# One planned order or the order of writing: the attention of a two-block kernel behind its scans

## The chip, the cores and the metric

The kernel runs on one core of a Trainium2 chip. The metric is the device time of one execution in microseconds (us); the figure given for a kernel is the median of its runs. A core has five engines with an instruction queue each: PE (TensorE, matrix products), DVE (VectorE), ACT (ScalarE), POOL (GpSimd) and SP (SyncE), which here issues nearly all DMA transfers. Engines meet through semaphores: an instruction can wait for another engine's or a DMA's.

## The reference

The input `x` is `[4, 96, 128, 128]` in float32. Two blocks follow each other, each on a group-normalised input and each added to its input.

Block 0 is a selective scan: a 1x1 product to 192 channels, a depthwise 3x3 convolution, SiLU, four scans over the image's pixels (rows, columns, and both backwards) with input-dependent decay, a layer norm over the channels and a product back to 96 channels.

Block 1, the one that the change concerns, in the reference's words:

```python
def _attn_conv(x1, x2, aw1, aw2, aw3):
    key = _unfold_nonoverlap(_conv2d(x1, aw1, pad), K).reshape(B, C, kk, -1)
    qry = _unfold_nonoverlap(_conv2d(x2, aw2, pad), K).reshape(B, C, kk, -1)
    attn = jnp.einsum('bckl,bqkl->bqck', key, qry)
    attn = jax.nn.softmax(attn.reshape(B, C, C * kk) / sqrt(C * kk), axis=2)
    value = _conv2d(x1, aw3, pad)
    return jax.vmap(lambda v, w: _conv2d(v[None], w, pad)[0])(value, w_attn)
...
xr, x1, x2 = _relu_split_norm(x, sc1, sc2, res_coef, nc1, nc2)
y1 = _layer_norm(_attn_conv(x1, x2, aw1, aw2, aw3))
y2 = _layer_norm(_conv2d(x2, w_conv2, K // 2)) * x1
return xr + _conv2d(jnp.concatenate([y1, y2], axis=1), w_full, 0) + b_full[None, :, None, None]
```

`_relu_split_norm` splits the normalised input into its positive part `x1` and negative part `x2`, each normalised with statistics over the whole image.

## The kernel before

**Stages.** The program first runs block 0: projections of the four images, and the scans (`ssm_scan`) over pairs of images. Beside the last scans it computes, for images 0 and 1, the scan output (`ssm_output`) and the norm (`split_norm`). Then block 1 follows image by image, `attention(img)`. While image b is in `attention`, a second generator runs beside it: the output of image b-1 (`attn_output`, by `close`), and, for b = 1 and 2, `ssm_output` and `split_norm` of image b+1. The output of image 3 runs alone at the end.

**How two stages are put side by side.** Each stage is a Python generator that emits instructions and yields a cost. `co_run(left, right, pace)` (line 275) takes a step of `left`, and then steps of `right` until these have cost `pace` times as much. In the attention the pace is 0.6 (line 1706). The order in which the Python code creates instructions is the order of emission.

**Attention.** An image has 11 strips of 12 rows. In a strip, two maps are convolved: `x1` (weights of key and value together) and `x2` (weights of query and `w_conv2` together), each in two chunks of 6 rows (q = 0, 1). The convolution uses four products for each pair of columns. For a chunk:
- `load_rows` (L1184 to L1195) loads rows in six DMAs, into one of two buffers;
- `columns`, a *turn* (L1201): sums and differences of neighbouring columns, on DVE (L1212 to L1214, L1219, L1221) and on POOL (L1212 to L1214), into one of three buffers;
- `products` (L1227): four PSUM banks, two large matmuls each (L1236), and then four small ones (L1247);
- `outputs` (L1262), a *combination*: ACT copies a bank (L1285), DVE forms two columns from four banks (L1277 to L1280), followed by statistics (L1377, L1508) and stores (L1392, L1412, L1509).

After the chunks q = 0 and 1, a third one (q = 2) does the remaining 64 output channels of both. Channels of key and query go into rings in SBUF. Whenever 9 rows are whole, *side pieces* follow the next chunks: transposes of the rings (`turned`, L1337, L1342) and the product of key and query (`multiplied`, L1352, added up by L1362). After 11 strips come softmax and the attention's weights, and then 22 chunks of the value convolution, whose order is the same (`wa` in place of `wd`).

The emission of a chunk is pipelined by hand. The turn of the next chunk comes first; then two matmuls for each bank, and between the banks `later.tick()` emits the copy, the combination, and the load and store that belong to earlier chunks. The banks come from a pool of six, `psa`; the work beside them has two others.

**What sets the order.** The program is written with a framework that tracks the dependences, and plans: it orders each engine's instructions by the emission and by what its own model of the durations holds ready, so an instruction that was emitted later may stand ahead of one emitted earlier. `in_order` (line 312) takes that freedom away for a part of the program: it makes every instruction depend on the one that was emitted before it on its engine. The dependence needs no semaphore, since an engine's own queue keeps its order.

```python
for i in traced()[first:]:
    if i.engine in before:
        tc.add_manual_dep(i, before[i.engine].name, ...)
    before[i.engine] = i
```

`first` is set at line 1670, after the projection of image 0. In the kernel before, `in_order(first)` is called at line 1691, so it covers the projections of images 1 to 3, the scans and what runs beside them. The attention, lines 1692 to 1709, is ordered by the planner.

**Output.** `attn_output` (L1515) begins with statistics (L180 to L190, L1536 to L1563: some 25 small operations, DVE, PE and ACT in turns), and goes on with 16 steps: three loads (L1569), ACT (L1578, L1582, L1588), DVE (L1583, L1584, L1589, L1590), and twice two matmuls (L1594, L1595) with a DVE addition (L1596), then a store (L1598).

Of the kernel before, what the change touches and what calls it, by code (L numbers as in the profile page):

```python
# [60 lines left out]
def kernel(  # L61
# [247 lines left out]
    def traced():  # L309
        return nc.cur_bb.bb.instructions  # L310

    def in_order(first):


        before = {}
        for i in traced()[first:]:
            if i.engine in before:
                tc.add_manual_dep(
                    i,
                    before[i.engine].name,  # L320
                    mybir.DependencyInfo(
                        mybir.DependencyClass.NoSync, mybir.DependencyReason.DATA
                    ),
                    reason="order of emission",
                )
            before[i.engine] = i
# [5 lines left out]
    def drain(gen):  # L332
        for _ in gen:
            pass
# [1328 lines left out]
    with tc.tile_pool(name="wp", bufs=1, side="left") as wp:  # L1663
# [6 lines left out]
        first = len(traced())  # L1670
# [17 lines left out]
    co_run(left, last, 1.6)  # L1688
    drain(left)
    drain(last)  # L1690
    in_order(first)
    early.close()
    psl = ctx.enter_context(tc.tile_pool(name="psa", bufs=6, space=PSUM, side="left"))
    psr = ctx.enter_context(tc.tile_pool(name="psr", bufs=2, space=PSUM, side="right"))
# [2 lines left out]
    for b in range(NB):  # L1697
# [9 lines left out]
        drain(left)  # L1707
        drain(light)
    drain(imgs[NB - 1].close(psr, "right"))


# [73 lines left out]
```

## Time and profile before

| what | value |
|---|---|
| median of 3 runs | 7653.22 us (7650.29 to 7659.47) |
| the profiled execution | 7650.29 us, span 7648.4 us |
| busy: PE, DVE, ACT, POOL | 5837.3 us, 5475.6 us, 3049.4 us, 3141.6 us |
| mean granted PE clock | 0.839 |

The stages behind the scans, in us from the span's start:

| stage | from | to |
|---|---|---|
| last scan instruction | | 3777 |
| image 0: keys and queries, softmax, values | 3788 | 4567 |
| image 1 (beside it the output of 0, scan output and norm of 2) | 4567 | 5636 |
| image 2 (beside it the output of 1, scan output and norm of 3) | 5636 | 6678 |
| image 3 (beside its first strips the output of 2) | 6678 | 7524 |
| output of image 3 | 7524 | 7648 |

A row of the view of busy time by stretch gives, for a window, how long each engine was executing. A row of the timeline gives start, duration, engine, line, operation, output and inputs; in brackets stands how long the engine had been idle before it, and the engine and instruction, or the DMA, that ended the idle time. A matmul in float32 shows as two records.

### The profile page before, as it was taken

To read this page: it belongs to the slowest core of one execution; us is meant where nothing else is said; L and a number is where in the kernel's file an instruction comes from. 1 tells how busy PE (TensorE), PEld (TensorE's weight loads), DVE (VectorE), ACT (ScalarE), POOL (GpSimd) and SP (SyncE) were. 2 spreads that over 40 slices of the span, in tenths; PEclk is the share of its full clock that TensorE was granted. 3 is DMA by queue.
4 is the path that set the end of the run, shared out by engine and by line. 5 is a ranking of instruction groups with operands and counts; after the bars stand their busy time and mean duration, and the time that the engine had idled before them with its cause. 6 is when DMAs were issued, how large, how long until landed. Compare 5 with 4: busy or idle time off the path is not lost. (4 is left out here: it accounts for less than half of the span.)

```text
span 7648.4 us, 72313 instructions
## 1 busy us (share of the span) xinstructions
PE 5837.3 (76%) x21940; PEld 2294.8 (30%) x21940; DVE 5475.6 (72%) x7531; ACT 3049.4 (40%) x3645; POOL 3141.6 (41%) x1826
## 2 busy tenths in 40 slices
PE   4989978789977535553588789987679886798877
PEld 1322322223211101110144433334334343344432
DVE  2248568788867795789866687457877567887678
ACT  1257566677854575376411102304213124121112
POOL 2038457668665465456722242112331112422231
PEclk9999989989965556655599899998899987899998
DMA  4566666766756655855544456586666776665445
GB/s 115 127 155 183 176 184 179 208 169 185 202 155 188 193 166 160 230 154 160 158 129 109 108 157 177 150 213 172 188 171 181 184 194 192 174 180 144 108 139 170
DMA packets 744604, 1279.07 MB, mean 167 GB/s; under 512 B 191654, under 2 KB 465730, under 8 KB 731736
## 3 DMA queue, kind: packets, MB, share of 16 engines
q1 hardware_dynamic: 742024, 1274.18, 60.5%
q8 instruction: 175, 2.87, 0.2%
q14 instruction: 213, 1.74, 0.1%
q0 software_dynamic: 2192, 0.27, 0.0%
HBM read 911.28 MB, written 295.13 MB: 158 GB/s over the span
## 5 line engine op out<-in xcount | busy, mean ns | idle before, releaser
L1236 PE MATMUL bank<-t,wd 128*128 128x384 f32 (+3 forms) x5632 | 1581.1, 512 | 289.8 <-DVE s L1278 118.4
L596 PE MATMUL bank<-y,wp 128*128 128x512 f32 (+3 forms) x3584 | 1323.5, 624 | 71.6 <-DMA y<-y 27.6
L1212 POOL TENSOR_TENSOR t<-y 128x768 f32<-128x768 f32 (+1 forms) x264 | 427.3, 1619 | 2285.8 <-PE bank L1236 1096.7
L826 POOL TENSOR_TENSOR y<-y,dl 128x1024 f32<-128x1024 f32 x384 | 1057.5, 2754 | 657.3 <-DVE dl L818 603.8
L770 PE MATMUL pBC<-xr,wbc 60*128 60x512 bf16 (+1 forms) x1536 | 651.0, 470 | 751.7 <-DVE dA L814 665.7
L793 POOL TENSOR_TENSOR dl<-dl,u 128x1024 f32<-128x1024 f32 x384 | 1034.0, 2693 | 463.1 <-ACT dA L761 293.9
L1285 ACT COPY s<-bank 128x384 f32<-128x384 f32 (+2 forms) x360 | 167.4, 465 | 2436.8 <-PE bank L1247 2318.8
L1236 PEld LDWEIGHTS bank<-t,wd 128*128 128x128 f32 (+1 forms) x5632 | 765.9, 176 | 1033.7 <-issue 610.9
L814 DVE TENSOR_TENSOR_SCAN dA<-dA,pBC 128x512 f32<-128x512 f32 x768 | 981.5, 1278 | 33.7
L818 DVE TENSOR_TENSOR dl<-dA,pBC 128x512 f32<-128x512 f32 x768 | 528.5, 688 | 298.1 <-PE pBC L770 225.6
L596 PEld LDWEIGHTS bank<-y,wp 128*128 128x128 f32 (+3 forms) x3584 | 460.8, 169 | 757.9 <-issue 646.3
L637 ACT ACTIVATE dl<-pd,dtb 128x512 f32<-128x512 f32 x768 | 485.6, 683 | 385.9 <-PE pd L744 382.7
L1236 PE MATMUL bank<-t,wa 128*96 128x384 f32 (+1 forms) x1408 | 494.3, 497 | 182.0 <-DVE s L1278 104.7
L797 DVE TENSOR_TENSOR pBC<-dl,pBC 128x512 f32<-128x512 f32 x768 | 526.6, 686 | 36.6 <-PE pBC L770 36.6
L1277 DVE TENSOR_TENSOR d<-s,bank 128x384 f32<-128x384 f32 (+2 forms) x360 | 191.9, 533 | 496.1 <-ACT s L1285 336.6
L770 PEld LDWEIGHTS <-wbc 60*128 60x128 bf16 (+1 forms) x1536 | 130.0, 103 | 1338.0 <-issue 1334.6
L1212 DVE TENSOR_TENSOR t<-y 128x768 f32<-128x768 f32 (+1 forms) x264 | 302.7, 1146 | 202.3 <-PE bank L1236 175.2
L761 ACT ACTIVATE dA<-dl,negA 128x1024 f32<-128x1024 f32 x384 | 420.2, 1141 | 2.3
L637 ACT ACT_TABLE_LOAD x239 | 306.6, 1283 | 264.8 <-PE pd L744 262.1
L1236 PEld LDWEIGHTS bank<-t,wa 128*96 128x96 f32 x1408 | 219.9, 168 | 451.1 <-issue 433.3
L744 PE MATMUL pd<-xr,wdt 60*128 60x512 bf16 (+1 forms) x768 | 308.8, 485 | 53.6 <-ACT dl L637 40.2
L969 PE MATMUL bank<-y,outws 96*96 96x512 f32 x512 | 340.3, 812 | 11.5 <-DMA y<-yms 11.4
(240 smaller groups left out, 7964.0 us busy)
## 6 DMA issues: line engine op xcount, KB each, us to landing
u<-zb SPq DMA_DIRECT2D x192, 1024.0 KB
y<-yms SPq DMA_DIRECT2D x128, 768.0 KB
xr<-xdt SPq DMA_DIRECT2D x768, 72.0 KB
yms<-y SPq DMA_DIRECT2D x96, 512.0 KB
xn<-xnew SPq DMA_DIRECT2D x128, 384.0 KB
y<-y SPq DMA_DIRECT2D x128, 258.2 KB
zb<-z SPq DMA_DIRECT2D x64, 512.0 KB
y<-x1d SPq DMA_DIRECT2D x168, 193.8 KB
```

What stands on the lines that cost most here:

```text
L596: nc.tensor.matmul(blocks(pz[p:e]), lhsT=ws[k][:, d, c : c + e - p], rhs=window(ys[k], at, d, n), start=(i == 0), stop=(i == len(terms) - 1),)
L637: nc.scalar.activation(dst, src, AF.Softplus, bias=bias)
L761: nc.scalar.activation(live[m]["dA"], live[m]["dl"], AF.Exp, scale=negA[:, g % 3, k : k + 1])
L770: nc.tensor.matmul(p, lhsT=wbc[0 : xr.shape[0], steps[n][0] % 3, q], rhs=xr[:, at : at + CH], start=True, stop=True,)
L793: nc.gpsimd.tensor_mul(t, t, u_view(n))
L797: nc.vector.tensor_mul(p, live[n]["dl"][:, bass.ts(half, CH)], p)
L814: nc.vector.tensor_tensor_scan(h, h, p, init, ALU.mult, ALU.add)
L818: nc.vector.tensor_mul(live[n]["dl"][:, sl], live[n]["dA"][:, sl], live[n]["C", half])
L826: nc.gpsimd.tensor_add(v, v, t.rearrange("p (a b) -> p a b", b=W))
L969: nc.tensor.matmul(po, lhsT=outws[:, j], rhs=y[:, j, sl], start=(j == 0), stop=(j == 1))
L1212: eng.tensor_sub(v[:, 0:2], of(y, 0), of(y, 2))
L1236: nc.tensor.matmul(pc[p:e, :n], lhsT=w[:, i, c : c + e - p], rhs=t[k][:, i, :n], start=(k == 0), stop=False,)
```

## The change

The call of `in_order(first)` moves from the end of the scans to the end of the program. The dependences along each engine now cover the attention, the work beside it and the last output too: each engine executes all that follows line 1670 in the order in which the Python code emits it. The same instructions are emitted, with the same pools, loads and sizes.

```diff
     co_run(left, last, 1.6)
     drain(left)
     drain(last)
-    in_order(first)
     early.close()
     psl = ctx.enter_context(tc.tile_pool(name="psa", bufs=6, space=PSUM, side="left"))
     psr = ctx.enter_context(tc.tile_pool(name="psr", bufs=2, space=PSUM, side="right"))
...
         drain(left)
         drain(light)
     drain(imgs[NB - 1].close(psr, "right"))
+    in_order(first)
```

## The prediction

> **What bounds the kernel now.** I read the busy time by stretch first. The change acts only behind the scans (last scan at 3777 us), and the stages there have different limits. Columns: window, length, then busy us (instructions) of PE, PE weight loads, DVE, ACT, POOL, then PE clock, DMA share, GB/s.
>
> ```profile
> 3788.00:4380.00 592.00, 495.54 (x2616) 261.10 (x2616) 385.13 (x605) 72.71 (x132) 172.16 (x151) 0.93 0.45 118
> 4380.00:4567.00 187.00, 141.74 (x537) 61.83 (x537) 160.57 (x250) 12.63 (x25) 75.30 (x59) 0.93 0.53 153
> 4575.00:4822.00 247.00, 222.43 (x813) 94.39 (x814) 194.28 (x258) 59.48 (x69) 60.68 (x48) 0.90 0.62 169
> 4840.00:5174.00 334.00, 299.16 (x1262) 124.42 (x1264) 163.75 (x281) 60.29 (x74) 42.80 (x43) 0.93 0.73 188
> 5201.00:5425.00 224.00, 166.90 (x852) 91.20 (x850) 167.27 (x281) 126.86 (x169) 55.70 (x73) 0.87 0.67 190
> 6920.00:7329.00 409.00, 355.42 (x1915) 190.40 (x1914) 269.68 (x425) 57.72 (x103) 114.49 (x100) 0.93 0.45 119
> ```
>
> Row 1 is the key and query convolutions of image 0, with no other work beside them; row 6 the same for image 3 once the output of image 2 is done. PE is 84 and 87% busy, so PE plus a stall. Row 2 is the value convolution (DVE 86% over the stretch, and almost gapless within it). Rows 3 to 5 are image 1 with, beside it, the output of image 0, the scan output of image 2 and the norm of image 2. Row 4 is PE work (90%).
>
> The timeline of a strip of image 3 shows the stall of rows 1 and 6. PE:
>
> ```profile
> 7125.08 1.48 PE L1236 MATMUL bank<-t,wd 128*128 128x384 f32 x4
> 7129.76 5.80 PE L1236 MATMUL bank<-t,wd 128*128 128x384 f32 x12 [3.20 <-DVE s L1278]
> ```
>
> and what DVE did meanwhile:
>
> ```profile
> 7122.10 0.96 DVE L1212 TENSOR_TENSOR t<-y 128x768 f32<-128x768 f32 x1 [2.05 <-PE bank L1236]
> 7122.98 1.83 DVE L1213 TENSOR_TENSOR t<-y 128x384 f32<-128x384 f32 x1
> 7124.73 1.18 DVE L1214 TENSOR_TENSOR t<-y 128x384 f32<-128x384 f32 x1
> 7125.83 1.58 DVE L1212 TENSOR_TENSOR t<-y 128x768 f32<-128x768 f32 x1
> 7127.33 0.54 DVE L1277 TENSOR_TENSOR d<-s,bank 128x384 f32<-128x384 f32 x1
> 7127.79 1.36 DVE L1213 TENSOR_TENSOR t<-y 128x384 f32<-128x384 f32 x1
> 7129.08 0.54 DVE L1278 TENSOR_TENSOR s<-s,bank 128x384 f32<-128x384 f32 x1
> ```
>
> The planner has put two column turns (L1212 to L1221) together, and L1278, which frees a PSUM bank, among them. PE stands 3.20 us in each 27.4 us half strip.
>
> One more wait counts, in the timeline at 7012 us: the write into the ring waits for the landing of the store of the chunk before, about 7 us after its issue.
>
> ```profile
> 7011.98 0.56 DVE L1279 TENSOR_TENSOR ring<-s,bank 128x384 f32<-128x384 f32 x1 [5.21 <-DMA c2d<-ring]
> ```
>
> **The Trainium skill.** "PSUM — Partial Sum Buffer", Engine vs sequencer instructions: the queues of ScalarE, VectorE and GpSimd are strictly first in, first out, and matmuls start in program order. So whatever stands ahead of a late instruction in the order costs it the wait; the last row above is an example, 5.21 us in which DVE did nothing else. "SBUF — State Buffer", SBUF: two separate sides: DVE operations with two SBUF inputs and GpSimd operations exclude each other on a shared port pair. The trace agrees: L1213 takes 1.83 us while POOL turns, 0.55 alone. "TensorE: Matmul & The Clock Gate", What's actually happening: after an idle window of some 3.4 us PE runs at half clock. The trace agrees in kind: pairs of L1594 records take 1.02 us in a dense stretch and 2.02 behind a wait at 4609 us.
>
> **The change part by part.** No instruction is added or removed. In the built programs the orders agree up to the attention; behind it, 4971 of DVE's 7469 instructions stand elsewhere, by 13 places on average, PE's and SP's less, POOL's hardly.
>
> *Strips with nothing beside them.* I laid out one strip (two maps, 6 chunks) in the new order with the durations of the rows: 8 matmuls of a chunk 5.35 us, the small ones 0.9, transposes 1.2, the product 1.7, a turn 4.56 (1.24+1.33+0.83+0.54+0.62, means of row 1's stretch), a combination 2.2 (four of 0.55), statistics 1.1, ACT copy 0.5. Where a side piece follows the third chunk, its combination now comes before the next turn: L1278 ends 3.6 us after the third chunk's last large matmul instead of 7. The second turn moves one chunk later. What is late next: in a half strip without side pieces the second turn stands before the first chunk's combination, so PE waits 4 us for that L1278; SP issues six loads (3.3 us) before the ring's store, which lands about 25 us into the half strip, and DVE stands 6 us at L1279. The two halves give 22.7+25.6 = 48.3 us; with about 0.1 us for a dozen handovers, 49.5. Before: 592/11 = 53.8 in image 0 and 409/7.8 = 52.3 in image 3. Gain: 11x4.3 = 47 and 7.8x2.8 = 22. Bounds: PE's own work (495/11 = 45 us a strip) gives 11x8.8+7.8x7.3 = 154; no gain gives 0.
>
> *Start of the first image.* Weights and maps are now issued after the last store of the scans; before, part of the weights went ahead. Some 8 issues at 0.4 to 0.8 us and a longer queue: +10 (0 to 20).
>
> *Image boundaries (three).* Before, the statistics chain of the output (bn_aggr to L1563, 4566 to 4581 us) ran while the new image's rows were loading, and PE's first convolution came at 4580. Now the first turn, which waits for the load to land (4578), stands ahead of that chain on DVE; the chain takes 10 us without what is mixed into it; and the output's own loads stand on SP behind a third row load that waits for that turn. All of PE's convolution is queued behind the first output matmul. +17 each, 51. Bounds: 0 and 30.
>
> *Output beside a convolution (three stages of 247 us).* DVE 194, PE 222. The first output matmul of each of 16 steps (L1595) now waits in place for DVE's L1584, 5 us of ACT and DVE work emitted just before it. In the old order PE could be given convolution meanwhile, and still lost 15 us there. +10 each, 30. Bounds: -10, and 3 us a step, 48.
>
> *Scan output and norm (images 1 and 2).* The scan output's statistics wait for a DMA (about 7 us) at the head of DVE: +8. The norm has two chains of some 20 to 40 small operations (5174 to 5201, 5290 to 5308), now unmixed: +10; but its strips gain as above, -15. The rest, in step with DMA at a share of 0.73: +5. Together +8 each, 16. Bounds: -20 and +40 each.
>
> *Value convolution (four times 187 us).* DVE is full in either order: 0 (-10 to +10 each).
>
> *Last output.* 16 steps, 124 us, DVE 94. SP now issues the next loads behind the store of the finished step, which waits for the last DVE operation: +8 (0 to 25).
>
> Sum: -47 -22 +10 +51 +30 +16 +8 = +46. Own time 7650.29 (span 7648.4): 7696. The median, 7653.22, lies 3 above it.
>
> **Rivals.** *The free strips win* (other side). If the ring's store lands in time and turns are shorter because they no longer collide with POOL, strips run at PE's 45.5 us: -91-53 instead of -69, total 7650+115-144 = 7621. It decides below 47.1 us a strip, where 11x(53.8-p)+7.8x(52.3-p) equals the 115 of losses. For it: row 1's PE idle is 96 us, nearly all behind L1278. Against it: the 5.21 us at L1279.
>
> *The mixed stages lose more.* If each of the 48 output steps costs PE 3 us (+144 instead of 30), and ACT's loads of the norm hold up its copies (64 x 0.5 us = 32): 7696+146 = 7842. For it: rows 3 to 5 have PE and DVE both near full, so strict order couples them. Against it: the planner's progress there (3.1 strips in row 3) is that of the emission order already (3.09 by its pace: 16 steps of 5.2 units over 0.6, at 45 units a strip), so little was rearranged.
>
> *No difference*: gains and losses cancel, 7650.
>
> **How the numbers follow.** A measurement here can tell about 0.2% (15 us). Moderate loss 0.44, strips win 0.24, large loss 0.20, no difference 0.12. Faster 0.24, same 0.12, slower 0.64. Range 7590 to 7810: it takes in the strips' case and most of the large loss. The likeliest case alone: 7666 to 7740.
>
> **What would show it.** Strips of image 0 at 47 to 51 us (key and query convolutions 520 to 560 instead of 592), with L1279 waiting for the ring's DMA more than 24 us in image 0; PE's wait for L1278 down. A boundary from the last value matmul to the first convolution of over 30 us instead of 16. More PE wait at L1595 for L1584 than 63 us. Wrong if free strips come to 46 us or if the mixed stages grow by over 40 us each.

## The result and the profile after

The kernel after takes 7851.08 us (median of four runs, 7843.54 to 7852.16), beside 7656.35 for the kernel before on the same chip: a ratio of 1.0251, interval 1.0233 to 1.0269. The span of its profiled execution is 7849.5 us, and the mean granted PE clock 0.824 instead of 0.839. The forecast was 7696 with a range up to 7810. The sign was as predicted, and so was the split into stages that gain and stages that lose. The size was not: the losses were some three times as large, in part through waits that the prediction did not price, and the time lies outside the range.

Beside the experiments below, the kernel before came to 7651 to 7666 us; a difference of under 15 us between two kernels is not read as one.

Busy time by stretch of the kernel after, with the stages of the rows shown of before, and in the last row the output of image 3 alone (columns as there):

```profile
3787.00:4328.00 541.00, 476.71 (x2580) 249.07 (x2580) 326.68 (x575) 60.41 (x118) 145.27 (x147) 0.95 0.45 121
4348.00:4518.00 170.00, 145.10 (x528) 62.18 (x528) 122.59 (x221) 10.08 (x22) 88.52 (x57) 0.94 0.60 165
4562.00:4814.00 252.00, 201.31 (x773) 88.19 (x772) 188.94 (x241) 62.68 (x68) 45.15 (x35) 0.88 0.58 159
4814.00:5194.00 380.00, 297.91 (x1298) 125.07 (x1297) 180.69 (x302) 62.45 (x79) 49.74 (x50) 0.85 0.68 177
5194.00:5474.00 280.00, 204.02 (x1011) 105.33 (x1010) 189.94 (x336) 135.78 (x178) 59.47 (x84) 0.85 0.61 171
7108.00:7484.00 376.00, 342.48 (x1935) 183.66 (x1919) 235.68 (x426) 47.74 (x93) 100.70 (x103) 0.98 0.46 122
7690.00:7849.50 159.50, 99.41 (x128) 30.51 (x126) 102.03 (x96) 56.43 (x47) 0.00 (x0) 0.67 0.52 143
```

Rows 1 and 6 are shorter, and PE's share rose to 88 and 91%. In rows 3 to 5 it fell to 80, 78 and 73%, where it had been 90, 90 and 75%. So the change does both things, each in its own stages. In the free strips (those with nothing beside them) PE's wait for L1278 fell, and DVE's wait for the ring's store grew. In the view of waits (us in total, times, longest us), image 0 in the kernel before:

```profile
PE bank L1236 <- DVE s L1278: 64.9, 19, 5.7
DVE ring L1279 <- DMA c2d<-ring: 24.3, 4, 7.4
```

and in the kernel after:

```profile
PE bank L1236 <- DVE s L1278: 35.4, 17, 9.5
DVE ring L1279 <- DMA c2d<-ring: 64.2, 9, 9.6
```

In image 3's free strips PE's wait for L1278 fell from 44.5 to 11.7 us; the ring's store is now the longer wait (a strip of image 3, DVE and PE):

```profile
7294.71 0.55 DVE L1278 TENSOR_TENSOR s<-s,bank 128x384 f32<-128x384 f32 x1
7298.63 0.55 DVE L1279 TENSOR_TENSOR ring<-s,bank 128x384 f32<-128x384 f32 x1 [3.37 <-DMA c2d<-ring]
7299.24 2.80 PE L1236 MATMUL bank<-t,wd 128*64 128x384 f32 x16 [1.71 <-DVE ring L1279]
```

Three groups of instructions carry the rest. Columns: line, engine, operation, tiles, count, then busy us and mean ns, then the idle time just before them and what ended it. In the kernel after:

```profile
L1236 PE MATMUL bank<-t,wa 128*96 128x384 f32 (+1 forms) x1408 | 502.4, 504 | 137.0 <-DVE s L1278 104.0 <-DMA wa<-watd 33.0
L969 PE MATMUL bank<-y,outws 96*96 96x512 f32 x512 | 365.3, 853 | 76.5 <-DMA y<-yms 76.5
L1595 PE MATMUL bank<-c,w 96*96 96x512 f32 x256 | 185.4, 815 | 212.8 <-DVE c L1584 212.8
```

The same three in the kernel before:

```profile
L969 PE MATMUL bank<-y,outws 96*96 96x512 f32 x512 | 340.3, 812 | 11.5 <-DMA y<-yms 11.4
L1236 PE MATMUL bank<-t,wa 128*96 128x384 f32 (+1 forms) x1408 | 494.3, 497 | 182.0 <-DVE s L1278 104.7 <-DMA wa<-watd 70.0 <-ACT s L1285 7.3
L1595 PE MATMUL bank<-c,w 96*96 96x512 f32 x256 | 150.4, 706 | 63.5 <-DVE c L1584 63.2
```

PE stood 149 us longer at the output's second matmul (L1595, for DVE's L1584), 65 us longer at the scan output's matmul (L969, for the load of `y`), and 37 us less for the weights of the value convolution.

How the order makes the wait at L1595 is seen in PE's timeline. Before, the planner had put convolution (L1247, L1236) between the two matmuls of a pair:

```profile
4627.91 1.10 PE L1594 MATMUL bank<-o,w 96*96 96x512 f32 x2
4628.94 0.92 PE L1247 MATMUL bank<-t,wd 32*128 32x384 f32 x4
4629.78 1.56 PE L1236 MATMUL bank<-t,wd 128*128 128x384 f32 x4
4631.18 1.02 PE L1595 MATMUL bank<-c,w 96*96 96x512 f32 x2
```

In the kernel after the second follows the first on PE, and nothing can be done while it waits:

```profile
4600.10 1.02 PE L1594 MATMUL bank<-o,w 96*96 96x512 f32 x2
4606.58 2.02 PE L1595 MATMUL bank<-c,w 96*96 96x512 f32 x2 [5.45 <-DVE c L1584]
```

Where the time went, by stage (starts and ends of the same instructions in the two traces):

| step of the prediction | predicted | before, us | after, us | measured |
|---|---|---|---|---|
| last scan operation on DVE to the first convolution | +10 | 14 | 18 | +4 (the scans ended 6 us earlier) |
| image 0, strips | -47 | 577.9 | 540.8 | -37 |
| image 3, free strips | -22 | 405.5 | 375.6 | -30 |
| last key and query matmul to first value matmul, 4 | not in the sum | 31.5, 42.8, 42.1, 30.9 | 20.8, 20.6, 20.8, 20.6 | -64 |
| value convolution, 4 | 0 | 674.7 | 680.1 | +5 |
| image boundary to first output addition, 3 | +51 | 21.2, 23.7, 23.2 | 44.9, 44.7, 43.8 | +65 |
| output beside a convolution, 3 | +30 | 236.8, 223.6, 223.3 | 251.5, 254.1, 249.8 | +72 |
| scan output and norm, to the last key and query matmul, images 1 and 2 | +16 | 594.0, 581.0 | 660.6, 660.9 | +147 |
| last output with the gap before it | +8 | 123.4 | 169.0 | +46 |

With the 6 us of the scans the rows add up to +201, the distance between the ends of the two spans. The gains (-131) are larger than predicted (-69); the losses are 3 times what was predicted.

The wait at L969 in the timeline of the kernel after (image 1). The load of `y` (L900) stands on SP behind the store of the ring (L1392), which waits for the combination (L1280). PE stands in place for its landing, and the convolution (L1236) behind it:

```profile
5066.68 0.55 DVE L1280 TENSOR_TENSOR ring<-d,bank 128x384 f32<-128x384 f32 x1
5067.25 0.79 SPq L1392 DMA_DIRECT2D vd<-ring  x2
5068.14 0.37 SPq L900 DMA_DIRECT2D y<-yms  x1
5072.92 3.70 PE L969 MATMUL bank<-y,outws 96*96 96x512 f32 x4 [5.58 <-DMA y<-yms]
```

### The profile page after: what moved, and what is told of

Same layout as the page of the kernel before. It is cut to its first block, busy times and chain, and to the rows that moved or that the text cites. A ratio compares the mean times of both kernels' runs of the same rounds, so it can differ in the third digit from the quotient of the medians.

```text
span 7849.5 us, 72432 instructions
## 1 busy us (share of the span) xinstructions
PE 5831.0 (74%) x21940; PEld 2279.5 (29%) x21940; DVE 5295.4 (67%) x7531; ACT 3052.0 (39%) x3645; POOL 3123.5 (40%) x1826
## 4 chain that ended last, share of the span: by engine, by line
PE 28%; DMA 28%; DVE 25%; ACT 8%; issue 5%; SPq 5%; POOL 0%; DVEq 0%; ACTq 0%; POOLq 0%
PE bank L596 9%; PE bank L1236 7%; DMA y<-vd 6%; DVE dA L814 5%; DMA y<-yms 4%; DMA xx<-xnew 2%; DVE pBC L797 2%; DVE half L1114 2%; PE bank L969 2%; DMA c2d<-ring 2%; DMA y<-x1d 2%; DMA xn<-xnew 2%; PE bank L918 2%; DVE dl L818 2%; PE pBC L770 2%
## 5 line engine op out<-in xcount | busy, mean ns | idle before, releaser
L1236 PE MATMUL bank<-t,wd 128*128 128x384 f32 (+3 forms) x5632 | 1592.5, 525 | 294.4 <-DVE s L1278 142.4
L1212 POOL TENSOR_TENSOR t<-y 128x768 f32<-128x768 f32 (+1 forms) x264 | 400.9, 1519 | 2695.8 <-PE bank L1236 2222.8
L596 PE MATMUL bank<-y,wp 128*128 128x512 f32 (+3 forms) x3584 | 1314.3, 622 | 67.9 <-DMA y<-y 27.7
L1236 PEld LDWEIGHTS bank<-t,wd 128*128 128x128 f32 (+1 forms) x5632 | 768.5, 179 | 1080.5 <-issue 594.7
L1236 PE MATMUL bank<-t,wa 128*96 128x384 f32 (+1 forms) x1408 | 502.4, 504 | 137.0 <-DVE s L1278 104.0
L969 PE MATMUL bank<-y,outws 96*96 96x512 f32 x512 | 365.3, 853 | 76.5 <-DMA y<-yms 76.5
L1213 POOL TENSOR_TENSOR t<-y 128x384 f32<-128x384 f32 (+1 forms) x264 | 352.7, 1336 | 0.0
L1595 PE MATMUL bank<-c,w 96*96 96x512 f32 x256 | 185.4, 815 | 212.8 <-DVE c L1584 212.8
```

Source lines behind the costliest of these rows:

```text
L596: nc.tensor.matmul(blocks(pz[p:e]), lhsT=ws[k][:, d, c : c + e - p], rhs=window(ys[k], at, d, n), start=(i == 0), stop=(i == len(terms) - 1),)
L969: nc.tensor.matmul(po, lhsT=outws[:, j], rhs=y[:, j, sl], start=(j == 0), stop=(j == 1))
L1212: eng.tensor_sub(v[:, 0:2], of(y, 0), of(y, 2))
L1236: nc.tensor.matmul(pc[p:e, :n], lhsT=w[:, i, c : c + e - p], rhs=t[k][:, i, :n], start=(k == 0), stop=False,)
```

## Experiments

**Where.** The first kernel keeps the order of emission only where nothing is emitted beside the attention.

```diff
-    def in_order(first):
+    def in_order(first, end):
...
-        for i in traced()[first:]:
+        for i in traced()[first:end]:
...
     drain(last)
+    in_order(first, len(traced()))
...
         co_run(left, light, 0.6)
+        alone = len(traced())
         drain(left)
+        in_order(alone, len(traced()))
         drain(light)
     drain(imgs[NB - 1].close(psr, "right"))
-    in_order(first)
```

> As the kernel before, but with the order of emission also in those parts of the attention that have nothing emitted beside them: all of image 0, and of images 1 to 3 what is left when the output, the scan output and the norm beside them are used up. The mixed stages and the last output stay with the planner. If the loss of the change comes from the stages in which two streams are mixed, and its gain from the others, this keeps the gain alone: image 0 -46, the gap at the softmax of images 1 to 3 about -20 each, free strips of image 3 -30, so about 7656 - 46 - 50 - 30 = 7530. If the stages can't be taken apart, because a stage that gains only hands its time to the next wait, it comes out at 7640 or more.

It took 7572.42 us: 0.990 of the kernel before (0.9885 to 0.9915). Image 0's strips take 546.2 us, image 3's free strips 373.4, the softmax gaps 21.8, 25.8, 26.0 and 21.9; the mixed stages and the last output are those of the kernel before (237.0, 222.1 and 219.4 us with the output; 103.7 at the end). So the stages can be taken apart: one edit holds a gain of some 80 us and a loss of some 275. The other 40 us that were expected went behind the norm: from the end of the output to the last key and query matmul, images 1 and 2 take 612.6 and 604.6 us instead of 594.0 and 581.0, which takes back what the gaps there gained.

**Whose instructions.** The second kernel holds all of the attention in order, but lets the planner place what runs beside it.

```diff
+    free = set()
+
+    def noted(gen):
+        while True:
+            at = len(traced())
+            got = next(gen, 0)
+            free.update(range(at, len(traced())))
+            if got == 0:
+                return
+            yield got
...
-        for i in traced()[first:]:
+        for at, i in enumerate(traced()[first:], first):
+            if at in free:
+                continue
...
-        light = chain(*light)
+        light = noted(chain(*light))
...
-    drain(imgs[NB - 1].close(psr, "right"))
+    drain(noted(imgs[NB - 1].close(psr, "right")))
```

> As the kernel after, but only the instructions of the attention itself are held in the order of emission; those of the output, the scan output and the norm that run beside it, and of the last output, may be placed by the planner. If the loss comes from waits of these instructions at the head of a queue, in the place where they were emitted, the mixed stages come back to the kernel before's length or below, the last output to about 107, and the total is 7500 to 7600. If it comes from the attention's own strict order (its loads on SP, its turns), which can't give way to the work beside it, the mixed stages stay near 912 and 915 us, and only the last output gains: about 7800.

7518.4 us, 0.9819 of before (0.9801 to 0.9837). The mixed parts of images 1 and 2, from the end of the output to the last key and query matmul, are 594.7 and 591.7 us instead of 661; the stages with the output 220.7, 219.2 and 221.2; the last output 106.3. The attention's own strict order costs little beside other work. The loss is that the work beside it stands where it was emitted.

**Which queue.** In four kernels one engine alone is freed from the order of emission behind the scans; two more free SP and PE together, and all but DVE. The edit, with the engines' names in its last line:

```diff
-    def in_order(first):
+    def in_order(first, free_from, free):
...
-        for i in traced()[first:]:
+        for at, i in enumerate(traced()[first:], first):
+            if at >= free_from and str(i.engine).endswith(free):
+                continue
...
     drain(last)
+    tail = len(traced())
...
-    in_order(first)
+    in_order(first, tail, "SP")
```

> As the kernel after, but in the attention SP alone may be ordered by the planner; PE, DVE, ACT and POOL keep the order of emission. If the loss is loads that are issued late because they stand on SP behind stores and loads that wait (L1569 behind L1598, the loads of the scan output and the norm behind L1392 and L1509), the last output comes from 149 back to about 110, each half of the scan output and each norm loses its waits for a DMA (image 1 and 2 about -50 each), and the total is about 7851 - 40 - 100 - 30 = 7680. If it is the engines that wait in place for each other, it stays within 30 us of 7851.

> As the kernel after, but in the attention PE alone may be ordered by the planner. If the loss is that matmuls of the convolution stand behind a matmul of the work beside them that waits (L1595 for L1584, L969 and L1236 for their inputs), the three stages with the output shrink by 15 to 30 each and the mixed parts of images 1 and 2 by 30 each, 7851 - 70 - 60 = 7720. If PE only waits for what comes late anyway, 7820 or more.

> As the kernel after, but in the attention DVE alone may be ordered by the planner. If turns and combinations stand on DVE behind work beside them that waits for PE, ACT or a DMA, 7750 to 7800; the free strips lose part of their gain (image 0 from 541 towards 578, +20, since the planner's placing of two turns together was on DVE). If DVE's order is not what costs in the mixed stages, the total rises to 7870 or more.

> As the kernel after, but in the attention ACT alone may be ordered by the planner. ACT is the least busy engine (63 us of 252 in the stage with the output), so if only long occupancy could delay others it changes nothing: 7851 within 20. If its copies of PSUM banks (L1285), which free the convolution, stand behind ACT operations that wait for a load (L910 72 us in one half, L1029 44, L1103 37), the mixed parts of images 1 and 2 shrink by 20 to 40 each: about 7790.

> As the kernel after, but in the attention both SP and PE may be ordered by the planner; DVE, ACT and POOL keep the order of emission. Alone, SP's freedom gave about -105 and PE's -127. If they are two separate losses (loads behind stores; convolution matmuls behind a waiting matmul), they add up: 7851 - 232 = 7620, the stages with the output near 220 and the last output near 107. If both are two ways round the same waits, the total stays at 7690 to 7720.

> As the kernel after, but in the attention only DVE is held in the order of emission. If the gain of the free strips is DVE's order alone, image 0 stays at 540 or below; if ACT's and POOL's freedom adds nothing, the total is that of the kernel with SP and PE free, within 20. If DVE's order costs as much in the mixed stages as PE's and SP's, it stays over 7700.

The second half of the scan output is counted from the first to the last L974.

| freed | us | output beside a convolution, 3 | second half of scan output, 2 | last output |
|---|---|---|---|---|
| none (after) | 7851.1 | 251.5, 254.1, 249.8 | 223.2, 223.6 | 148.8 |
| SP | 7743.6 | 244.1, 249.2, 245.1 | 209.7, 207.2 | 127.6 |
| PE | 7724.1 | 228.7, 226.6, 224.3 | 216.9, 216.9 | 135.2 |
| DVE | 8006.1 | 263.5, 267.3, 262.5 | 234.2, 228.0 | 152.9 |
| ACT | 7851.4 | 250.6, 251.0, 252.5 | 224.0, 226.1 | 147.6 |
| SP and PE | 7584.4 | 218.5, 214.1, 216.1 | 201.3, 200.9 | 101.1 |
| all but DVE | 7608.3 | 212.0, 216.3, 212.3 | 204.1, 203.4 | 98.5 |

SP's freedom gives 107 us, PE's 127, both together 267: two losses on two queues, and a little more. (Not all of the 267 is loss taken back: with both free, image 0's strips come to 524 us instead of 541.) What stands on PE in the wrong place is felt most in the stages with the output, what stands on SP in the scan output and at the end. ACT's gives nothing, although ACT waited 72.2 us for loads of the scan output in one of its halves; the idle time was not on the path. DVE's freedom alone cost 155 us: image 0's strips went from 541 to 570 us, as predicted, but the mixed stages grew too (251.5 to 263.5). Why the planner's order on DVE alone is worse there than its order on all engines, no run shows. Freeing ACT and POOL besides SP and PE adds nothing: that kernel is 24 us slower than the one with SP and PE free, a little more than the 20 us that were allowed for.

**The output's own wait.** In the kernel "a step ahead", the ACT and DVE part of step t+1 is emitted behind step t's addition, so that a piece of convolution is emitted between L1584 and L1595; its loads (`load(t, ...)` issues those that are named) follow the last use of their buffer. In "loads early" only the loads move.

```diff
+            def front(t):
...
+                load(t + 2, "xx")
+                ready[t] = o, c2, e
...
             for t in range(NS):
-                o, c2, xx = ahead
-                if t + 1 < NS:
-                    ahead = loads(t + 1)
...
+                o, c2, e = ready.pop(t)
...
                     nc.vector.scalar_tensor_tensor(e[:, sl], pf, lb, e[:, sl], ALU.add, ALU.add)
+                    if h:
+                        load(t + 2, "o", "c2")
+                        nc.sync.dma_start(ob[:, bass.ts(t, SN)], e)
+                        front(t + 1)
                     yield 2.6
-                nc.sync.dma_start(ob[:, bass.ts(t, SN)], e)
```

> As the kernel after, but the output works a step ahead: ACT's and DVE's part of step t+1 (L1578 to L1590) is emitted before the convolution work that stands ahead of its matmuls, and the loads for t+2 follow at once behind the last use of their buffer instead of at the start of the next step. If L1595's wait for L1584 and the loads behind the store are what the output loses, the three stages with the output beside a convolution shrink by 15 to 30 us each (252, 254, 250 to about 230), and the last output from 149 to about 110: in all -85 to -130, about 7740. If these waits only stand where another wait would (DVE is 75% busy there), the three stages stay within 5 us and only the last output gains: about 7810.

> As the kernel after, but of the output's step only the loads move: for t+2 they are emitted right behind the last use of their buffer, ahead of the store of the step. If the last output is slow because its loads stand behind that store, it comes from 149 to 115 or less, and the stages with the output stay within 8 us of 252, since L1595 still waits there for L1584: about 7815. If the loads are the cause in those stages too, all of the gain of the kernel that works a step ahead comes with them: 7755.

A step ahead: 7753.23 us, 98 less than the kernel after; the stages with the output 225.1, 226.2 and 220.5, the last output 124.0, and PE's wait at that matmul 67.9 us instead of 212.8. Loads early: 7819.21; the stages with the output 248.9, 248.3 and 249.7, the last output 125.0. So at the end it is the loads, and beside a convolution it is the matmul that stands for L1584. The end in the kernel after, from the timeline (store, the three loads behind it, and ACT, which waits for the last of them):

```profile
7738.65 0.32 SPq L1598 DMA_DIRECT2D out<-e  x1
7739.06 0.38 SPq L1569 DMA_DIRECT2D o<-od  x1
7739.53 0.66 SPq L1569 DMA_DIRECT2D c<-c2d  x1
7740.28 0.45 SPq L1569 DMA_DIRECT2D xx<-xnew  x1
7747.36 1.24 ACT L1578 ACTIVATE xx<-xx,b,rstd 96x1024 f32<-96x1024 f32 x1 [7.78 <-DMA xx<-xnew]
```

The load of `xx` issued at 7740.28 lets ACT begin at 7747.36, 7.1 us later, and another 11.4 us pass until that step's store: two buffers, so two steps in some 20 us. The same place in the kernel before, where `xx` is loaded as soon as its buffer's last reader (L1590) is done, ahead of the matmuls and the store, and ACT begins 3.5 us after the load's issue:

```profile
7568.23 1.27 DVE L1590 SCALAR_TENSOR_TENSOR e<-xx,low,e 96x1024 f32<-96x1024 f32 x1
7569.57 0.30 SPq L1569 DMA_DIRECT2D xx<-xnew  x1
...
7572.91 0.32 SPq L1598 DMA_DIRECT2D out<-e  x1
7573.11 1.24 ACT L1578 ACTIVATE xx<-xx,b,rstd 96x1024 f32<-96x1024 f32 x1 [3.71 <-DMA xx<-xnew]
```

**The scan output's load.** The load of `y` for step c+2 moves up, to right behind the last matmul that reads its buffer (in the second half alone).

```diff
                         nc.tensor.matmul(
                             po, lhsT=outws[:, j], rhs=y[:, j, sl], start=(j == 0), stop=(j == 1)
                         )
+                    if h and c + 2 < NS:
+                        ahead.append(load_y(c + 2))
```

> As the kernel after, but in the second half of the scan output the load of y for step c+2 is emitted right behind the last matmul that reads its buffer, ahead of the stores and row loads of the convolution that come until the next step. If PE's wait at L969 for that load, with the convolution's matmuls behind it, is what lengthens this half, it comes from 223 to 205 or less in images 1 and 2, and the total falls by about 35 to 7815. If it is something else (DVE's L974 and L1279 waiting for stores to land), it stays within 6 us of 223.

7823.01 us. The second half fell from 223.2 and 223.6 to 196.7 and 203.5 us, which is the kernel before's 199.4 and 197.1. PE's wait for the load in the half of image 1 is 8.3 us instead of 33.2 (in the view of waits: us in total, times, longest us; the kernel after first, then this one):

```profile
PE bank L969 <- DMA y<-yms: 33.2, 9, 6.3
```

```profile
PE bank L969 <- DMA y<-yms: 8.3, 3, 4.3
```

So the place of this load is a cause of that half's length, worth 26.5 and 20.1 us here; DVE's waits for stores in the same half (L1279: 28.8, then 26.4 us) stayed, so this gain didn't come from them. It isn't the only thing that sets the length: in the kernel "statistics first" below, the half of image 1 takes 200 us although PE's wait for the load is still 26.0 us, with 676 matmul records in it instead of 725.

The total fell by 28 us only. The edit also moves the load in the scan output of images 0 and 1, which runs beside the scans; there the scans ended 17 us later than in the kernel after, and the first convolution began at 3804.9 us instead of 3786.8.

**The image boundary.** Of three kernels the first two missed what was expected, and the third came in part. First, two chunks of the new image ahead of the output:

```diff
         left = imgs[b].attend(psl)
+        for _ in range(11 if b else 0):
+            next(left)
         co_run(left, light, 0.6)
```

> As the kernel after, but the first two chunks of an image's convolution are emitted before the first step of the work beside it (images 1 to 3). If the boundary lost 27 us because the output's statistics and first matmul stand in front of the convolution on PE, it comes down from 44 to about 20 and the total falls by about 20 x 3 = 60, to 7790. If the boundary is set by the landing of the new image's rows, it stays at 40 or more and the total within 10 us of the kernel after.

7890.07 us, slower than the kernel after. PE's first convolution comes 9.5 us after the last value matmul, but then:

```profile
4543.11 1.62 PE L1236 MATMUL bank<-t,wd 128*128 128x384 f32 x2 [9.10 <-DVE t L1213]
4568.04 2.90 PE L1236 MATMUL bank<-t,wd 128*128 128x384 f32 x4 [8.82 <-DVE s L1278]
4590.48 2.02 PE L1595 MATMUL bank<-c,w 96*96 96x512 f32 x2 [5.54 <-DVE c L1584]
```

It stands 8.82 us, because the combination (L1278) is on DVE behind a turn whose rows are still landing; and the statistics, which had run while rows landed, follow with nothing beside them. The first output addition comes 59 us after the last value matmul instead of 45. Next, the statistics, and with them the output's first loads and its first half step, ahead of the first turn:

```diff
             load(0)
             load(1)
+            yield 0.0
             turn(0)
...
         left = imgs[b].attend(psl)
+        next(left)
+        if b:
+            next(light)
         co_run(left, light, 0.6)
```

> As the kernel after, but in images 1 to 3 the output's statistics, its first loads and its first half step are emitted between the image's first two row loads and the first turn, and so stand ahead of the turn on DVE and ahead of the third row load on SP. If the boundary is long because the statistics and the output's loads stand behind the first turn, which waits for the rows, the time from the last value matmul to the end of the output's stage (296, 299, 293 us for about 3.0 strips) falls by about 20 each, and the total by 60, to 7790. If the landing of rows and loads sets it, it stays within 6 us each.

7844.13 us, and 38.6, 40.1 and 40.3 us to the first convolution instead of 43.8, 44.0 and 43.1: the theory fell. The statistics were done by 4534.5, and PE then stood for the output's load of `o` (its lines stand one further on than in the kernel after):

```profile
4545.64 2.02 PE L1595 MATMUL bank<-o,w 96*96 96x512 f32 x2 [11.20 <-DMA o<-od]
4552.63 2.02 PE L1596 MATMUL bank<-c,w 96*96 96x512 f32 x2 [4.97 <-DVE c L1585]
```

In the kernel before, the planner had moved these loads up, as its timeline shows:

```profile
3865.42 0.42 SPq L1569 DMA_DIRECT2D xx<-xnew  x1
4547.86 0.92 SPq L1569 DMA_DIRECT2D o<-od  x2
```

The two loads of `o` are issued 16 us before the last value matmul (4563.6); those of `c` and `xx` are issued between 3865 and 3919 us, beside image 0's own convolution. ACT and DVE do the first two steps up to L1590 there as well (L1590 at 3881.71 and 3910.22), all but L1584, which needs the statistics. At the boundary nothing was left to land but the rows. (Some 7 us of DVE's work so stood in image 0's strips before, and stand behind the boundary in the kernel after.) So in the third kernel the loads for steps 0 and 1 are emitted before the last value strip as well:

```diff
             for s in range(nstrip):
+                if s == nstrip - 1:
+                    next(img.closing)
...
+            ahead = [loads(0), loads(1)]
+            yield 0.0
             so, _ = combine(ps, img.ost.rearrange("p c s -> p (c s)"), mean96, "so")
```

> As the kernel with the statistics first, and besides the output's loads for its steps 0 and 1 are emitted before the last strip of the value convolution that precedes it. If the landing of these loads sets the boundary, the first matmul of the output comes right behind the statistics (16 us after the last value matmul), the first convolution 6 us later: the boundary falls from 44 to 22 us, the total by about 60 to 7790 or, with the last output's first loads hidden too, 7780. If rows landing or the order on PE sets it, the boundary stays at 35 or more.

7815.1 us. The boundary is 27.5, 27.8 and 27.5 us, and the first output matmul follows the statistics without a wait (lines four further on):

```profile
4541.31 2.00 PE L1598 MATMUL bank<-o,w 96*96 96x512 f32 x2
4545.58 2.02 PE L1599 MATMUL bank<-c,w 96*96 96x512 f32 x2 [2.27 <-DVE c L1588]
```

The loads and the place of the statistics together make 16 of the 27 us. Whether the other 11 are ACT's and DVE's part of the first steps, which the planner had also moved ahead, was not tested. But the stage with the output then takes 261 to 264 us instead of 250 to 254, with some 0.2 strip less of convolution done (542 instead of 577 of L1236's records for keys and queries, 192 to a strip): the third load of rows is now behind. Of the time from the last value matmul to the end of that stage (296.4, 298.8 and 293.6 us) only 10, 9 and 6 us were saved. In both of these kernels another part of the gain came from a stage that they don't touch: the second half of the scan output takes 200 and 202 us instead of 223. Why is not shown; half a step of the output has moved, and other pieces of the convolution fall into that half.

**Both.** Last, the planner places what runs beside the attention, and the output works a step ahead as well.

> As the kernel with only the attention held in order and the work beside it left to the planner (7518), with the output working a step ahead as before. If the planner has already put DVE's part of a step ahead of its matmuls, it changes nothing: 7518 within 15. If waits at L1595 are left, 15 us in each of the three stages: 7475.

7469.53 us, 0.9749 of the kernel before (0.9732 to 0.9766), and the fastest of all. The stages with the output take 197.2, 200.2 and 204.2 us, the last output 99.9. The expectation of 15 us a stage was a little low (23.5, 19 and 17). Row 3's stage in this kernel:

```profile
4551.00:4748.50 197.50, 178.50 (x769) 79.74 (x767) 169.87 (x233) 58.50 (x63) 46.09 (x40) 0.99 0.72 202
```

Nearly the same matmuls as in row 3 of the kernel after (769 and 773 records), at a granted clock of 0.99 instead of 0.88: PE is busy 178.5 us instead of 201.3.

## Why the prediction was wrong

*What held.* The stall behind L1278 in the free strips was real, and emission order takes about half of it away in image 0 and most of it in image 3: image 0's strips came to 49.2 us (predicted 49.5), image 3's to 47.0. PE's wait for L1278 in image 0's strips fell from 64.9 to 35.4 us. That DVE would then stand at L1279 for the ring's store held too: 64.2 us in image 0 instead of 24.3. The value convolution stayed within 7 us each and came to 5 us more in all. The boundary was over 30 us. The rival in which the strips win needed 47.1 us a strip and 115 us of losses; the strips gave it in image 3 and not in image 0, and the losses were three times as large. Its ground, that row 1's 96 us of idle PE are "nearly all behind L1278", was misread: 64.9 us of them are; 12.9 are behind L1279, and 8.5 lie already in the softmax gap. (409/7.8 is 52.4 and not 52.3 us a strip, which changes nothing.) The sign named for being wrong came: the mixed stages of images 1 and 2 grew by 81 and 110 us.

*The step that failed first: that in the mixed stages the planner's progress "is that of the emission order already", "so little was rearranged".* It was used to set the rival aside, and the output stages stayed at +10 each. It didn't fit the prediction's own count either, by which 4971 of DVE's instructions stand elsewhere, by 13 places on average. The progress was nearly the same (3.1 strips before, 3.0 after), but the place of each L1595 within a step was not. Where the planner had put a piece of convolution between L1584 and L1595, emission put none: 212.8 us of waiting instead of 63.5. The rival's 3 us for each of 48 output steps, 144, came as a wait of 149, of which 33 are in the last output (19.2 before, 52.6 after) and the rest in the three images. The stages themselves lost 72 us, within the step's upper bound of 48 a stage. The step-ahead kernel takes the wait down to 67.9 us and, beyond it, the time of those stages to 220 to 226.

*The largest miss: scan output and norm, at +8 each.* It was 67 and 80 us. The prediction priced the statistics and the chains of small operations at the head of DVE, and called the rest "in step with DMA": +5. It did not ask what stands in front of the loads on SP. There each load of `y` is behind a store that waits for DVE; PE stands for it in place, with the convolution behind: 76.5 us at L969 instead of 11.5. Moving that one load gave back the half's 27 and 20 us. With SP and PE free, the halves take 201 us. The norm's part was not tested by itself: its two parts of image 1 take 260 us before, 264 after and 252 with SP and PE free. Another 35 us in each image are strips that were done beside the norm before, which ended 18.7 and 18.4 us behind the last key and query matmul, and now follow it alone for 16.5. The discounted part of the rival, "ACT's loads of the norm hold up its copies", fell: freeing ACT changed nothing.

*Last output: +8, bound 25; measured 42, or 46 with the gap before it.* The step named the right queue ("SP now issues the next loads behind the store of the finished step"). It took the delay of the issue once and left out that, with two buffers, the landing (7.1 us) and the step's own chain follow one another in every second step.

*Boundary: +51, measured +65.* The order of events was right, the weights were not: the chain of statistics counted for less than the landing of the output's loads, which the prediction named ("the output's own loads stand on SP behind a third row load") and did not price. That the planner had fetched some of them 650 us earlier I had not looked up.

*Not in the sum: the softmax gap, -64.* The prediction took the value stage as unchanged and left out what lies ahead of it. In the kernel before, the planner put most of a turn of the value convolution and half of a second ahead of the maximum (L1475) on DVE, and row loads ahead of the weights on SP; in image 0, from the weights' store to their reload passed 7.5 us there and 3.2 after. Emission order has the chain first. In images 1 and 2 the end of the norm fell into the gap as well (18.7 and 18.4 us of it), so a part of their gain there is the other side of the strips above.

So the losses were under-read by a common fault: I priced the order on DVE with care, and the orders of SP and PE hardly at all. The Trainium skill, "PSUM — Partial Sum Buffer", Engine vs sequencer instructions, calls the queues of ScalarE, VectorE and GpSimd strictly first in, first out, and says that matmuls start in program order. I used it for DVE's rows, while the two queues whose order costs time here are PE's (127 us alone) and SP's (107). Of SP's queue that section says nothing; its price is this case's own.

## What to carry to other kernels

Hold one stream in the order in which it was written by hand, and leave the work that fills its gaps movable: in this kernel the order was worth 132 us when it bound the attention alone, and cost 195 when it bound everything. Before fixing an order, list for every matmul of the guest stream what it waits for and how many instructions lie between, and for every load what stands in front of it on the issuing queue; a load behind a store that waits for an engine is late by that engine. Where a wait remains, emit the producer one step ahead of its consumer, so that the written order leaves room between them.

## What the runs showed of the hardware

A stall cost PE twice here. In row 3's stage PE's busy time for 769 to 773 matmul records was 201.3, 198.9 and 178.5 us at granted clocks of 0.88, 0.91 and 0.99 (kernel after, the one with the work beside it free, and the one that is a step ahead as well). The 54.5 us between the first and the last are so 22.8 of slower matmuls and 31.7 of PE's idle time. The Trainium skill, "TensorE: Matmul & The Clock Gate", What's actually happening, names idle windows as what lowers the clock. This case agrees in kind: a pair of L1595 records took 2.02 us behind a wait (at 4606.58 us in the kernel after, shown above) and 1.02 in a dense stretch (at 4631.18 in the kernel before). No run changes the clock by itself.

The same load took 3.5 us or 7.1 us, by what was issued around it. The Trainium skill, "DMA: Bandwidth & Descriptors", Anatomy of one DMA, fits 2.0 us and bytes over 436e3 (for transfers issued by GpSimd), an estimate of 2.9 us for 393 216 bytes (384 KB); here, for loads issued by SP, ACT could begin 3.5 us after the issue of `xx` at 7569.57 us in the kernel before, with no other issue for 6 us before it and 2.5 us behind it, and 7.1 us after the issue at 7740.28 in the kernel after, the last of three such loads behind a store, all within 2 us. So the figure for one transfer is near the first and a poor price for the second. That the neighbours are the cause is likely, and not tested by itself.
